# A last batch whose verdict is formed by a minimum, whose statistics and bias additions are placed between other work, and whose last block of rows is stored first

## The chip, the core and the metric

The kernel runs on one core of one Trainium2 chip. The core has five engines that run at the same time and wait for each other through semaphores: TensorE (PE, matrix products), VectorE (DVE), ScalarE (ACT), GpSimd (POOL) and SyncE (SP, which issues the DMAs of this kernel). The metric is the device time of one execution in microseconds (us), lower is better. Several executions are timed, and the median is given. One further execution is recorded by the profiler. Its span runs from the first to the last instruction, and all positions below are microseconds from the start of that span.

## The reference

The input `x` holds 32 batches of 512 rows with 512 columns in float32, `adj` is a 512x512 matrix of zeros and ones. Two layers follow each other, each a graph operation whose result is added to its input and normalised row by row.

```python
# layer 0: attention with 8 heads of 64, masked by adj
q, k, v = x @ Wq + bq, x @ Wk + bk, x @ Wv + bv
scores = einsum('bihd,bjhd->bhij', q, k) / sqrt(64)
scores += where(adj == 0, -1e9, 0)
x = layernorm(x + einsum('bhij,bjhd->bihd', softmax(scores), v))
# layer 1: neighbours summed by adj, one product with a weight, a bias
y = einsum('nm,bmd->bnd', adj, x)
x = layernorm(x + einsum('bnd,do->bno', y, weight) + bias)
# layernorm(x) = (x - mean) / sqrt(var + 1e-5) over the 512 columns
```

## The kernel before

A batch stays in SBUF as one tile of 128 partitions with four row blocks of 128 rows, called `xs` in the profile, or `xT` for the last batch. In the code it is `X[b]`, and block `c` is `X[b][:, c, :]`. Products of 512x512 matrices (the projections, and `convolve`, which multiplies the aggregated rows `YT[b]`, tile `yT`, by the weight of layer 1) are made by a scheme with seven products of quarter matrices instead of eight. `FACTORS` lists, for each of the seven, which quarter or sum of quarters stands on the left and on the right. `ORDER` and `convolution` name the order in which they are issued, for layer 1 it is 1, 2, 5, 6, 7, 3, 4. Each product is eight matmuls at line 353. The quarters A11 and A12 of the left factor are copied from PSUM, S1 is added by DVE, and S2, S3 and S4 are three POOL additions (`combine_rows`, line 318).

The order of work is written out by hand: each engine works through its instructions in program order, and the semaphores are put in from the tiles (and the parts of tiles) that an instruction reads and writes. The main loop interleaves batches. The projections of a batch run beside the attention of the one before, and layer 1 runs one batch behind again.

After the loop (line 816 on) only the end of two batches is left. With `t` = 31, the last batch, these are the steps that the change touches, in their order before:

- `rest` is layer 1 of batch 30, seven `convolve` units. A unit makes eight matmuls, after which DVE adds the PSUM bank to quarters of `X[30]` (line 534) or to a mixed sum `MIX` (line 530), and for products 6, 7 and 4 POOL adds `MIX` to a quarter (line 532, for product 4 line 537). Product 7 writes the same `MIX` tile that POOL reads for product 6.
- `ahead` is the first normalisation of batch 31. For each row block `c`, ACT normalises the block (line 430), ACT rounds it to a high part (line 491), and DVE subtracts to get the low part (line 492). Then comes the next unit of `rest`. High and low parts are the weights of `aggregate_rows`, the product with `adj`.
- `older` is the second statistics of batch 29, four pairs of `bn_stats` and `bn_aggr` on DVE (lines 415 and 416).
- `add_bias` adds the bias row of layer 1 to one block of batch 31 on POOL (line 495). It overwrites the block that the high and low parts are made from, and layer 1's products are added to it later.
- `judge` condenses three checks on sums that were gathered during the run to one number per partition: three reductions (lines 662 to 664), two comparisons (666, 667) and two multiplications (668, 669) on DVE. A small matmul at line 873 and a comparison at line 874 make of it the verdict, which decides at the end of the program whether a slower general kernel is run afterwards.
- `aggregate_rows` makes 32 matmuls (line 504) into four banks, row block by row block, and copies them to `yT`. ACT copies banks 0 and 2 (line 511), DVE copies banks 1 and 3 (line 509), and DVE adds for S1 (line 513).
- `last` is layer 1 of batch 31, its seven products interleaved with the second normalisation of batches 29 (`old`) and 30 (`seen`, `next_`) and with their stores. The end normalises and stores batch 31 block by block: blocks 0 and 1, then block 2 by ACT (line 430) and block 3 by DVE (line 887), each stored by a DMA of 256 KB on SP's queue (line 454).

Of the kernel before, what the change touches and what calls it, by code (L numbers as in the profile page):

```python
# [37 lines left out]
FP = mybir.dt.float32  # L38
# [4 lines left out]
ALU = mybir.AluOpType  # L43
AX = mybir.AxisListType
# [3 lines left out]
P = 128  # L48
# [147 lines left out]
def gnn_resnorm_kernel(tc, *args):  # L196
    nc = tc.nc
    with tc.tile_pool(name="verdict", bufs=1) as keep:
        verdict = keep.tile([1, 1], I32, name="verdict")
        fast_kernel(tc, verdict, *args)  # L200
        amiss = nc.values_load(verdict[0:1, 0:1], min_val=0, max_val=1,
                               skip_runtime_bounds_check_because="it is a comparison's result, 0 or 1")
        with tc.If(amiss > 0):
            general_kernel(tc, *args)
# [3 lines left out]
def fast_kernel(ctx: ExitStack, tc, verdict, x, adj, Wq, bq, Wk, bk, Wv, bv, W1, b1, out):  # L208
    nc = tc.nc
# [3 lines left out]
    NB = N // P  # L213
# [4 lines left out]
    consts = ctx.enter_context(tc.tile_pool(name="consts", bufs=1))  # L218
# [233 lines left out]
    def store(b, blocks=None):  # L452
        for c in blocks or ():
            nc.sync.dma_start(out[b, c * P:(c + 1) * P, :], X[b][:, c, :])
        if blocks is None:
            nc.sync.dma_start(out[b].rearrange("(c p) d -> p c d", p=P), X[b])
# [24 lines left out]
    def split_rows(b, c):  # L481

        if c > 1:
            both = work.tile([P, 2, D], FR, name="k", bufs=2)
            high, low = both[:, 0, :], both[:, 1, :]
        else:
            high = work.tile([P, D], FR, name="high")
            low = work.tile([P, D], FR, name="low")
        HIGH[b, c], LOW[b, c] = high, low
        row = X[b][:, c, :]  # L490
        nc.scalar.activation(high, row, AF.Copy)
        nc.vector.tensor_sub(low, row, high.bitcast(FP))

    def add_bias(b, c):
        nc.gpsimd.tensor_add(X[b][:, c, :], X[b][:, c, :], b1_r)
# [48 lines left out]
    def convolution(b):  # L544
        return [(convolve, b, i) for i in (1, 2, 5, 6, 7, 3, 4)] if b >= 0 else []
# [114 lines left out]
    def judge():  # L660
        seen = consts.tile([P, 3], FP, name="seen")
        nc.vector.tensor_reduce(seen[:, 0:1], sums, axis=AX.XY, op=ALU.add)
        nc.vector.tensor_reduce(seen[:, 1:2], inverses, axis=AX.XY, op=ALU.add)
        nc.vector.tensor_reduce(seen[:, 2:3], inexact, axis=AX.X, op=ALU.add)
        well = consts.tile([P, 3], FP, name="well")
        nc.vector.tensor_scalar(well[:, 0:2], seen[:, 0:2], BOUND, None, op0=ALU.is_le)
        nc.vector.tensor_scalar(well[:, 2:3], seen[:, 2:3], 0.0, None, op0=ALU.is_equal)
        nc.vector.tensor_mul(well[:, 0:1], well[:, 0:1], well[:, 1:2])
        nc.vector.tensor_mul(well[:, 0:1], well[:, 0:1], well[:, 2:3])
        return well[:, 0:1]  # L670


    def run(units):
        for unit in units:
            unit[0](*unit[1:])
# [46 lines left out]
    def norm(t, which):  # L722

        if t - which < 0:
            return []
        lo, hi = which * NB, (which + 1) * NB
        return [(square_root, t, slice(lo, hi)), (invert_root, t, slice(lo, hi))] + [
            (normalise, t, slot) for slot in range(lo, hi)]
# [4 lines left out]
    def survey(b):  # L733

        return [(statistics, b, 1, c) for c in range(NB)] if b >= 0 else []
# [81 lines left out]
    t = B - 1  # L817
    rest, last = convolution(t - 1), convolution(t)
# [5 lines left out]
        statistics(t, 0, c)  # L824
    ahead = norm(t, 0)
    run(ahead[:1] + rest[1:2] + ahead[1:2])
    for c in range(NB):
        run(ahead[2 + c:3 + c])
        split_rows(t, c)
        run(rest[2 + c:3 + c])  # L830
    run(rest[2 + NB:])
    older, seen = survey(t - 2), survey(t - 1)
    run(older)
    for c in range(NB):
        add_bias(t, c)
    well = judge()
    aggregate_rows(t)
    old = norm(t - 1, 1)
# [40 lines left out]
    for c in (2, 3):  # L879
# [6 lines left out]
    row = X[t][:, 3, :]  # L886
    nc.vector.tensor_scalar(row, row, STAT[t + 1][:, NB + 3, 0:1], RSTD[t + 1][:, NB + 3:NB + 4],
                            op0=ALU.subtract, op1=ALU.mult)
    store(t, [2, 3])


# [22 lines left out]
```

## Time and profile before

| what | value |
|---|---|
| median of 3 executions | 2749.52 us (2749.11 to 2749.98) |
| the profiled execution | 2749.17 us |
| its span | 2747.3 us |
| PE busy | 2729.7 us, 99% |
| DVE, POOL, ACT busy | 2064.8, 1903.0, 1411.4 us |
| mean granted clock of PE | 0.998 |
| start of `rest` and `ahead` in the span | about 2699 us |

The time outside the span (2749.17 less 2747.3, so 1.87 us) lies before the first and after the last instruction. A row of the timeline gives start, duration, engine, line, operation, output and input with their shapes, and in brackets how long the engine stood idle before it and what ended that. On DVE a row's duration overlaps the next one's by some 0.08 us, so that the distance from start to start is the cost of one more instruction.

### The profile page before, as it was taken

Reading aid. Unit: us, or ns where it says so; the run is one execution under the profiler, and the core shown is the slowest. Engines: PE = TensorE matmul, PEld = TensorE weight load, DVE = VectorE, ACT = ScalarE, POOL = GpSimd, SP = SyncE. Lnnn points to the kernel's source line nnn. Section 1 sums busy time; section 2 is a strip of 40 time slices with the busy share of each in tenths; the row PEclk is TensorE's granted clock in tenths of the full one; section 3 lists DMA queues with packets and bytes.
Section 4 is the critical chain, followed back from the end, with each engine's and each line's share of the span. In section 5 each row is a group of like instructions: output and inputs, shape, how many; then the busy total and the mean of one; then the engine's idle time right before and its main releaser. Section 6 shows DMA issues by size and latency. Waiting matters only on the chain.

```text
span 2747.3 us, 39383 instructions
## 1 busy us (share of the span) xinstructions
PE 2729.7 (99%) x12856; PEld 1911.3 (70%) x12856; DVE 2064.8 (75%) x3348; ACT 1411.4 (51%) x2459; POOL 1903.0 (69%) x1224
## 2 busy tenths in 40 slices
PE   9999999999999999999999999999999999999997
PEld 6676676766767767667676676676766767767666
DVE  6777777777777787777877777777777777777777
ACT  3455464554544655446555455454554644555454
POOL 4776677666867667777677676777666867667775
PEclk9999999999999999999999999999999999999999
DMA  5212211222212222122221222211222212222121
GB/s 149 32 28 62 56 29 45 57 62 57 44 30 56 61 59 54 19 57 60 60 57 23 51 59 61 56 27 47 58 62 57 43 30 56 62 58 49 25 59 50
DMA packets 592915, 142.20 MB, mean 52 GB/s; under 512 B 554560, under 2 KB 558656, under 8 KB 592704
## 3 DMA queue, kind: packets, MB, share of 16 engines
q1 hardware_dynamic: 592704, 139.63, 23.0%
q8 instruction: 103, 1.69, 0.3%
q14 instruction: 108, 0.88, 0.1%
HBM read 72.88 MB, written 33.55 MB: 39 GB/s over the span
## 4 chain that ended last, share of the span: by engine, by line
PE 98%; DVE 1%; DMA 0%; ACT 0%; issue 0%; SPq 0%; POOL 0%; DVEq 0%; ACTq 0%
PE bank L353 56%; PE bank L561 17%; PE bank L585 16%; PE bank L472 8%; PE bank L628 0%; DMA wq<-in_L_gnn_Wq_dram 0%; DVE bnst L415 0%; DVE xs L534 0%; DVE part L847 0%; PE bank L287 0%; POOL xs L532 0%; SPq L239 0%; ACT xT L430 0%; DVE stat L416 0%; DVE xT L534 0%
## 5 line engine op out<-in xcount | busy, mean ns | idle before, releaser
L565 ACT ACTIVATE e<-e 128x1024 f32<-128x1024 f32 x512 | 524.9, 1053 | 572.8 <-DVE e L563 537.5
L563 DVE SCALAR_TENSOR_TENSOR e<-gap,bank 128x512 f32<-128x512 uint8 x1024 | 617.7, 679 | 20.2 <-PE bank L561 20.2
L576 POOL TENSOR_TENSOR es<-es,e 128x1024 f32<-128x1024 f32 x256 | 618.3, 2415 | 20.1
L576 POOL TENSOR_TENSOR es<-e 128x1024 f32<-128x1024 f32 x128 | 316.2, 2470 | 328.2 <-ACT e L565 328.2
L561 PE MATMUL bank<-q,k 64*128 64x512 f32 x2048 | 463.0, 598 | 0.0
L585 PE MATMUL bank<-e,v 128*64 128x512 f32 x2048 | 453.6, 595 | 0.0
L353 PE MATMUL bank<-wv,xT 128*128 128x256 f32 x1792 | 405.4, 381 | 0.0
L353 PE MATMUL bank<-xT,wk 128*128 128x256 f32 x1792 | 402.9, 379 | 0.0
L353 PE MATMUL bank<-xT,wq 128*128 128x256 f32 x1792 | 400.8, 381 | 1.9 <-DMA wq<-in_L_gnn_Wq_dram 1.7
L353 PE MATMUL bank<-w,yT 128*128 128x256 f32 x1792 | 394.3, 380 | 3.5 <-DVE yT L509 3.5
L561 PEld LDWEIGHTS bank<-q,k 64*128 64x128 f32 x2048 | 203.4, 186 | 258.0 <-issue 152.2
L353 PEld LDWEIGHTS bank<-w,yT 128*128 128x128 f32 x1792 | 341.2, 191 | 52.0 <-DVE yT L509 3.9
L353 PEld LDWEIGHTS bank<-xT,wk 128*128 128x128 f32 x1792 | 340.2, 190 | 46.1
L353 PEld LDWEIGHTS bank<-xT,wq 128*128 128x128 f32 x1792 | 337.8, 190 | 48.9 <-issue 1.9
L353 PEld LDWEIGHTS bank<-wv,xT 128*128 128x128 f32 x1792 | 337.6, 190 | 47.6 <-DVE e L563 0.8
L644 ACT ACTIVATE rows<-rows,zero,inverse 128x64 f32<-128x64 f32 x1008 | 343.4, 427 | 4.6 <-DMA rows<-attT 4.6
L585 PEld LDWEIGHTS bank<-e,v 128*64 128x64 f32 x2048 | 141.4, 137 | 277.1 <-issue 275.7
L648 POOL TENSOR_TENSOR xs<-xs,rows 128x512 f32<-128x512 f32 x124 | 158.0, 1285 | 164.3 <-DMA xs<-in_x_dram 164.3
L565 ACT ACT_TABLE_LOAD x30 | 38.5, 1283 | 416.6 <-DVE e L563 416.6
L445 DVE TENSOR_TENSOR low<-xs,high 128x512 fp32r<-128x512 f32 x122 | 141.8, 1162 | 106.1 <-ACT high L441 106.1
L534 DVE TENSOR_TENSOR xs<-bank,xs 128x512 f32<-128x512 f32 x186 | 124.3, 682 | 96.8 <-PE bank L353 46.2
L430 ACT ACTIVATE xs<-xs,shift,rstd 128x512 f32<-128x512 f32 x248 | 181.9, 803 | 27.2 <-DVE shift L425 27.2
(128 smaller groups left out, 2963.3 us busy)
## 6 DMA issues: line engine op xcount, KB each, us to landing
rows<-attT SPq DMA_DIRECT2D x2016, 16.0 KB, 1.8
xin<-in_x_dram SPq DMA_DIRECT2D x496, 64.0 KB, 2.4
xs<-in_x_dram SPq DMA_DIRECT2D x31, 1024.0 KB, 5.1
out_dram<-xs SPq DMA_DIRECT2D x31, 1024.0 KB, 4.4
xin<-in_x_dram SPq DMA_DIRECT2D x4, 256.0 KB, 3.3
wq<-in_L_gnn_Wq_dram SPq DMA_DIRECT2D x2, 512.0 KB, 6.7
wk<-in_L_gnn_Wk_dram SPq DMA_DIRECT2D x2, 512.0 KB, 5.7
yT<-in_adj_dram SPq DMA_DIRECT2D x1, 1024.0 KB, 7.2
```

Source lines behind the costliest of these rows:

```text
L353: nc.tensor.matmul(pm[:, r, :], left[:, d, r * P:(r + 1) * P], right[:, d, :], start=(d == 0), stop=(d == 1))
L430: nc.scalar.activation(row, row, AF.Identity, bias=SHIFT[t][:, slot:slot + 1], scale=RSTD[t][:, slot:slot + 1])
L445: nc.vector.tensor_sub(LOW[b, d], cols, HIGH[b, d].bitcast(FP))
L472: nc.tensor.matmul(pm.rearrange("p a n -> p (a n)"), part, adjT[:, n % NB, :], start=(n == 0), stop=(n == 2 * NB - 1))
L534: nc.vector.tensor_add(block, pm, block)
L561: nc.tensor.matmul(ps[s], keys[:, j * P:(j + 1) * P], queries, start=True, stop=True)
L563: nc.vector.scalar_tensor_tensor(e[:, s, :], gap[:, j, :], NEG * root, ps[s], op0=ALU.mult, op1=ALU.add)
L565: nc.scalar.activation(e, e, AF.Exp, scale=1.0 / root)
L576: nc.gpsimd.tensor_add(ES[b, hp], ES[b, hp] if j > 1 else E[b, hp, 0], E[b, hp, j])
L585: nc.tensor.matmul(po[s * HD:(s + 1) * HD, :], values, e[:, s, :], start=(j == 0), stop=(j == NB - 1))
L644: nc.scalar.activation(part, part, AF.Identity, bias=zero, scale=inverse[:, c, s:s + 1])
L648: nc.gpsimd.tensor_add(cols, cols, ROWS.pop((b, hp)))
```

## The change

- `judge` makes one reduction with a minimum over its three columns in place of the two multiplications, into a fourth column of the tile `well`.
- The additions of bias to the four blocks of batch 31 are issued within the loop over `c`: for block 0 right after the low part, for blocks 1 to 3 after the unit of `rest` that follows the low part.
- Two of the four statistics of batch 29 are issued in the loop at `c` = 2, after the low part and ahead of product 7. The other two stay after the last unit of `rest`.
- The last two stores are issued in the order block 3, block 2.

```diff
-        well = consts.tile([P, 3], FP, name="well")
+        well = consts.tile([P, 4], FP, name="well")
         nc.vector.tensor_scalar(well[:, 0:2], seen[:, 0:2], BOUND, None, op0=ALU.is_le)
         nc.vector.tensor_scalar(well[:, 2:3], seen[:, 2:3], 0.0, None, op0=ALU.is_equal)
-        nc.vector.tensor_mul(well[:, 0:1], well[:, 0:1], well[:, 1:2])
-        nc.vector.tensor_mul(well[:, 0:1], well[:, 0:1], well[:, 2:3])
-        return well[:, 0:1]
+        nc.vector.tensor_reduce(well[:, 3:4], well[:, 0:3], axis=AX.X, op=ALU.min)
+        return well[:, 3:4]
...
     run(ahead[:1] + rest[1:2] + ahead[1:2])
+    older, seen = survey(t - 2), survey(t - 1)
+
     for c in range(NB):
         run(ahead[2 + c:3 + c])
         split_rows(t, c)
+        if c == 0:
+            add_bias(t, c)
+        if c == 2:
+            run(older[:2])
         run(rest[2 + c:3 + c])
-    run(rest[2 + NB:])
-    older, seen = survey(t - 2), survey(t - 1)
-    run(older)
-    for c in range(NB):
-        add_bias(t, c)
+        if c > 0:
+            add_bias(t, c)
+    run(rest[2 + NB:] + older[2:])
     well = judge()
     aggregate_rows(t)
...
-    store(t, [2, 3])
+    store(t, [3, 2])
```

## The prediction

> **What bounds the kernel now.** The page came first: PE is busy 99% of 2747.3 us at a mean clock of 0.998, so only places where PE stands still or runs slowly can give anything before PE's end, and after it the chain of the last batch. The waits of PE over the whole run name one such place at the end:
>
> ```profile
> PE bank L353 <- DVE yT L509: 3.5, 1, 3.5
> ```
>
> The columns are total, count and longest. It is one wait. The chain of work that ended last (start, duration, what) shows what PE waits for, namely `judge`, of which two multiplications of one column take 2.4 us:
>
> ```profile
> 2719.50 0.48 DVE well L666
> 2719.98 0.06 DVE well L667
> 2720.04 1.16 DVE well L668
> 2721.20 0.02 issue
> 2721.22 1.18 DVE well L669
> 2722.41 0.61 DVE yT L509
> 2723.02 0.04 issue
> 2723.07 10.16 PE bank L353 x38
> ```
>
> The timeline of DVE and POOL tells why such small instructions are slow, and gives the prices used below:
>
> ```profile
> 2711.91 1.68 POOL L532 TENSOR_TENSOR xs<-xs,mix 128x512 f32<-128x512 f32 x1 [8.48 <-DVE mix L530]
> ...
> 2713.62 0.69 DVE L530 TENSOR_TENSOR mix<-bank,mix 128x512 f32<-128x512 f32 x1 [1.19 <-POOL xs L532]
> ...
> 2717.44 4.96 POOL L495 TENSOR_TENSOR xT<-xT,b_r 128x512 f32<-128x512 f32 x4
> ...
> 2719.28 0.16 DVE L663 TENSOR_REDUCE seen<-inverses 128x1 f32<-128x16 f32 x1
> ...
> 2719.90 0.14 DVE L667 TENSOR_SCALAR well<-seen 128x1 f32<-128x1 f32 x1
> ...
> 2722.33 0.68 DVE L509 COPY yT<-bank 128x512 f32<-128x512 f32 x1
> ```
>
> The four bias additions run back to back from 2717.44, 1.24 us apart, so they end near 2718.7, 2719.9, 2721.2 and 2722.4. Lines 666, 668 and 669 end at 2719.98, 2721.20 and 2722.40: each waited for the POOL addition in flight. The reductions and line 667 did not. DVE also stood idle 1.19 us before line 530 (product 7 behind POOL's line 532).
>
> Last, the granted clock of PE, by stage (length, busy of the engines, then PEclk, DMA share, GB/s):
>
> ```profile
> 2719.00:2721.00 2.00, 0.58 (x3) 0.17 (x1) 1.97 (x8) 0.32 (x1) 2.00 (x2) 1.00 0.00 0
> ...
> 2723.00:2724.00 1.00, 0.93 (x4) 0.86 (x5) 1.00 (x4) 0.00 (x0) 0.00 (x0) 1.00 0.00 0
> 2724.00:2725.00 1.00, 1.00 (x5) 0.77 (x4) 0.27 (x1) 0.18 (x1) 0.59 (x1) 0.67 0.00 0
> 2725.00:2726.00 1.00, 1.00 (x4) 0.82 (x3) 0.48 (x1) 0.60 (x2) 1.00 (x2) 0.50 0.00 0
> 2726.00:2727.00 1.00, 1.00 (x4) 0.82 (x3) 0.97 (x4) 0.04 (x1) 1.00 (x2) 0.50 0.00 0
> 2727.00:2728.00 1.00, 1.00 (x4) 0.79 (x4) 0.96 (x3) 1.00 (x2) 1.00 (x1) 0.62 0.00 0
> ```
>
> After the gap the clock falls to a half for some 3 us, which costs 0.33 + 0.50 + 0.50 + 0.38 = 1.7 us of PE's work.
>
> **What the Trainium skill says.** "SBUF — State Buffer", Who interferes with whom: DVE and GpSimd share a pair of ports as an exclusive lock; a DVE instruction with two SBUF inputs, or a one-input one in a two-port mode, waits for a running GpSimd instruction that reads SBUF, while `tensor_reduce` never does. The trace agrees: the multiplications waited 1.1 us each, the reductions took 0.14 to 0.16 us under a busy POOL. "VectorE: DVE Perf Modes", Mode 2×_2P: the two-port mode wants an even outermost dimension (or an odd one equal on both sides). Line 666 (two columns) waited; line 667 (one column) did not, so here the measurement decides. "TensorE: Matmul & The Clock Gate", What's actually happening: after an idle window of about 3.4 us the clock is halved. The 3.5 us gap and the 0.50 after it fit.
>
> **The change, part by part.** Durations are start to start: 0.60 us for a DVE operation on 512 columns, 0.80 for a statistics pair (2716.02 to 2716.84), 1.24 for POOL. One that finds the pair taken starts when it is released.
>
> *Bias of block 0.* It can start at 2709.51, after the low part ends at 2709.43, and ends at 2710.78. The low part of block 1, due at 2710.55, waits for it and ends at 2711.33 instead of 2711.23: 0.10 us later, and so is line 530 of product 6 (ends 2711.93). POOL's line 532 waits for DVE's low part of block 2, as before (the 1.68 above), and ends at 2713.69; bias 1 behind it ends at 2714.93.
>
> *Two statistics ahead of product 7.* They fill 2712.45 to 2714.05. Line 530 needed POOL's 2713.69, so 1.60 us of work replaces a wait that was 1.19: it then runs to 2714.73. If that cover were gone they would simply cost their 1.60 here and save 1.60 later.
>
> *Low part of block 3.* It is ready at 2714.65 but bias 1 holds the pair to 2714.93: it ends at 2715.50 against 2714.91. PE reaches block 3's matmuls after 24 of 32, 2711.31 + 24 x 0.233 = 2716.9, so 1.4 us of cover remain.
>
> *POOL afterwards.* The addition of product 7 starts when the low part lets go (2715.41) and ends at 2716.65, bias 2 at 2717.89, bias 3 at 2719.13, line 537 of product 4 at 2720.37. Line 537 comes later than before (2717.48); its reader is the statistics of batch 30, more than 5 us further on.
>
> *DVE afterwards.* Products 3 and 4 take 2715.42 to 2716.62, the other two statistics end at 2718.22, three reductions and an issue bring line 666 to 2718.47. There it meets bias 3 and waits until 2719.13, 0.66 us. Its price is thus 0 to 1.24 us by where it falls in a POOL addition; my sum gives 0.66. Line 667 and the minimum follow at 0.12 each (667 to 668 was 0.12), so the copy of line 509 starts near 2719.35 instead of 2722.33. The minimum is a form not seen before; the reductions of line 664 (0.07 to 0.12 start to start) and the page's word that it never waits bound it at 0.07 and, if it did wait, 1.24.
>
> *PE.* The matmul after the copy starts 0.74 us behind it (2722.33 to 2723.07), so at 2720.09. The gap shrinks from 3.50 to 0.5 us, too short for the clock to fall.
>
> *What is late next.* From the copy on DVE sets the pace, not PE: it is busy almost without a break from 2725.5 to 2735, its line 530 for product 6 starts at 2733.24 long after product 6 was made, and product 3's addition at 2735.37 waited 0.60 for the POOL addition behind that. PE's own product 3 ended at 2735.28, so both arrived together. Ahead of that DVE is tied to POOL's S2 to S4 additions: line 425 waited for the second of them to end, and these follow DVE's copies by a fixed distance (POOL is free from 2720.37, they are due at 2721.4). So everything behind the copy moves by 2722.33 - 2719.35 = 2.98 us, stores of batches 29 and 30 on SP's queue included, and the 1.7 us of clock become slack of PE.
>
> *Stores.* Block 3 is ready at 2741.08 (DVE, line 887), block 2 at 2741.53 (ACT). Before, SP issued at 2741.55 and 2741.98. Now it issues block 3 at about 2741.1 and block 2 at 2741.55, 0.43 us earlier for the last. But instruction fetches (the rows q8 and q14 of the DMA part of the page) run on some of the same DMA engines at that moment[...]. Between 0 and 0.43, I take 0.2.
>
> *Sum:* 2.98 + 0.2 = 3.2 us. The profiled execution took 2749.17 (span 2747.3 and 1.87 around it), so 2746.0 for it; the median shown is 0.35 above it, so 2746.3.
>
> **Rivals.** A change of 0.2% is 5.5 us (about what a measurement of this kernel can tell from no change): a faster time outside it would be below 2744.0.
>
> 1. *One POOL addition more.* Line 666 or the minimum misses bias 3 and waits for line 537, to 2720.37. For it: DVE has only 0.66 us in hand, and line 667 may take the pair too. Against: it did not before. Gain 3.2 - 1.24 = 2.0, so 2747.5.
> 2. *PE is the bound to the end.* Then the clock counts: 3.0 + 1.7 + 0.2 = 4.9, so 2744.6. For it: PE and POOL arrived within 0.1 us at product 3. Against: DVE's unbroken chain.
> 3. *Starvation.* POOL keeps the pair while it has work, and the low part of block 3 waits for two additions more, to 2718.0. Then the copy comes near 2721.3, gain 1.2, 2748.3. Against: lines 666 and 668 got in at the next boundary with POOL's queue full.
> 4. *Slower.* `well` grows by 4 bytes per partition, which can move the tiles laid out after it. If operands at other addresses made each of PE's 12,856 matmuls 3.2 us / 12,856 = 0.25 ns longer, the gain would be gone; 0.5 ns gives 2752.7. Nothing in the profile shows a cost by address.
> 5. *Nothing.* The copy is held by something not seen, 2749.5. Against: its bank is complete near 2718.3, between ACT's copies at 2717.84 and 2718.72.
>
> **How the numbers follow.** My forecast (2745.3 to 2747.0) 0.66; rival 1 0.13; rival 2 0.10; rival 3 0.05; rival 4 0.03; rival 5 0.03. The range 2744.8 to 2748.2 takes in the forecast, rival 1, part of 2 and part of 3. Faster by over 0.2% is the lower edge of rival 2, 0.04; slower by over 0.2% the upper edge of rival 4, 0.01; the rest, 0.95, lies within.
>
> **What would show it.** PE's wait for line 509 at 0.3 to 0.8 us, a granted clock of 1.00 in the twelve us after it, no row of `well` but line 666 above 0.2 us, no idle time of DVE before product 7's line 530, the copy near 2719.35, the last DMA issue near 2738.6. A PE wait of 1.5 us or more speaks for rivals 1 or 3; a tail from the copy to the last DVE instruction shorter than before (18.75 us, 2722.33 to 2741.08) for rival 2; PE's matmuls in the main loop longer than before for rival 4. Wrong would be a copy that starts earlier while the end does not.

## The result and the profile after

The changed kernel takes 2745.82 us (median of 22 executions, 2744.52 to 2747.74) against 2750.36 us for the kernel before (22 executions, 2748.33 to 2753.43). The ratio is 0.9983, with a 95% interval from 0.9978 to 0.9989, so 4.5 us less, with 3.0 to 6.1 us inside the interval. The forecast was 2746.3 us and 3.2 us less. The profiled execution took 2744.69 us, its span 2742.9 us.

The waits of PE over the whole run, of the changed kernel (total, count, longest):

```profile
PE bank L353 <- DVE yT L509: 0.5, 1, 0.5
```

Before, this wait was 3.5 us. The chain of work that ended last, of the changed kernel (start, duration, what), shows the judgement without its long rows. Line 668 is now the minimum. Behind the copy the chain leaves PE after the six matmuls that complete product 1, passes ACT's copy of it (line 524) and is mostly DVE's from there on, where it had stayed with PE for 10 us:

```profile
2717.43 0.69 DVE well L666
2718.12 0.07 DVE well L667
2718.19 0.02 issue
2718.21 0.16 DVE well L668
2718.37 0.61 DVE yT L509
2718.98 0.04 issue
2719.02 1.58 PE bank L353 x6
2720.60 0.02 issue
2720.62 0.61 ACT mix L524
```

The timeline of POOL and DVE of the changed kernel, the rows that answer to those shown of before:

```profile
2710.95 1.67 POOL L532 TENSOR_TENSOR xs<-xs,mix 128x512 f32<-128x512 f32 x1 [1.23 <-DVE mix L530]
...
2713.01 0.67 DVE L530 TENSOR_TENSOR mix<-bank,mix 128x512 f32<-128x512 f32 x1
...
2713.83 1.76 POOL L532 TENSOR_TENSOR xs<-xs,mix 128x512 f32<-128x512 f32 x1
...
2717.40 0.72 DVE L666 TENSOR_SCALAR well<-seen 128x2 f32<-128x2 f32 x1
2718.03 0.14 DVE L667 TENSOR_SCALAR well<-seen 128x1 f32<-128x1 f32 x1
2718.21 0.16 DVE L668 TENSOR_REDUCE well<-well 128x1 f32<-128x3 f32 x1
2718.28 0.68 DVE L509 COPY yT<-bank 128x512 f32<-128x512 f32 x1
```

DVE no longer stands idle before line 530 of product 7, the minimum takes 0.16 us while POOL works, and of the judgement only line 666 waits for POOL, once. The granted clock by stage (length, busy of the engines, PEclk, DMA share, GB/s) stays at full speed behind the short gap:

```profile
2718.00:2719.00 1.00, 0.51 (x3) 0.11 (x1) 0.97 (x5) 0.25 (x1) 1.00 (x2) 1.00 0.00 0
2719.00:2720.00 1.00, 0.98 (x5) 0.88 (x6) 1.00 (x3) 0.00 (x0) 0.32 (x1) 1.00 0.00 0
2720.00:2721.00 1.00, 1.00 (x6) 0.90 (x5) 0.22 (x1) 0.38 (x1) 0.63 (x1) 1.00 0.00 0
2721.00:2722.00 1.00, 1.00 (x7) 0.87 (x6) 0.68 (x2) 0.40 (x2) 1.00 (x2) 1.00 0.00 0
2722.00:2723.00 1.00, 1.00 (x6) 0.88 (x5) 0.97 (x4) 0.08 (x1) 1.00 (x2) 1.00 0.00 0
```

Positions in two profiles can't be compared from the start of the span, because the work ahead of the change differs from execution to execution by about as much as the change is worth. T0, the start of the first low part of batch 31 (line 492), lies at 2708.74 us in the first profile of before, at 2707.68 us in that of the changed kernel, and between 2707.68 and 2711.75 us over all profiles of this study. A part of this spread is the clock at the start of the run: in the four profiles with T0 beyond 2710 us (e1, e4, e6 and the second one of the changed kernel) the granted clock falls to a half between 8 and 16 us, in the other ten it does not. From T0 the two stand like this (the length of a span is read to 0.1 us, so its end is good to 0.05 us):

| from T0, us | before | changed | difference |
|---|---|---|---|
| copy of line 509 starts | 13.59 | 10.60 | 2.99 |
| from there to the end of DVE's last instruction | 18.75 | 18.68 | 0.07 |
| from there to the end of the span | 6.22 | 5.94 | 0.28 |
| end of the span | 38.56 | 35.22 | 3.34 |

The spans of these two profiles differ by 4.4 us; 1.06 us of that is the difference in T0, ahead of anything the change touches.

### The profile page after: what moved, and what is told of

Read it like the earlier page. It is cut to its first block, busy times and chain, and to the rows that moved or that the text cites. A ratio compares the mean times of both kernels' runs of the same rounds, so it can differ in the third digit from the quotient of the medians.

```text
span 2742.9 us, 39381 instructions
## 1 busy us (share of the span) xinstructions
PE 2728.6 (99%) x12856; PEld 1911.0 (70%) x12856; DVE 2063.2 (75%) x3347; ACT 1411.1 (51%) x2459; POOL 1903.8 (69%) x1224
## 3 DMA queue, kind: packets, MB, share of 16 engines
q8 instruction: 103, 1.69, 0.3%
## 4 chain that ended last, share of the span: by engine, by line
PE 98%; DVE 1%; DMA 0%; ACT 0%; issue 0%; SPq 0%; POOL 0%; DVEq 0%; ACTq 0%
PE bank L353 56%; PE bank L561 17%; PE bank L585 16%; PE bank L472 8%; PE bank L628 0%; DVE bnst L415 0%; DMA wq<-in_L_gnn_Wq_dram 0%; DVE xT L534 0%; DVE xs L534 0%; DVE part L850 0%; DVE stat L416 0%; DVE mix L530 0%; PE bank L287 0%; SPq L239 0%; ACT xT L430 0%
```

## The experiments

Each was profiled once, and all but the last also timed against the kernel before. The table gives what the profile of each shows. "Tail" is from the start of the copy to the end of DVE's last instruction, "end" is the end of the span from T0, and the last column is the median less that of the kernel before in the same comparison. The intervals of these differences reach some 2 us to each side, so the verdicts on single parts rest on the positions.

| kernel | copy | PE's wait | tail | last DVE to end | end | median difference |
|---|---|---|---|---|---|---|
| before | 13.59 | 3.5 | 18.75 | 6.22 | 38.56 | |
| changed | 10.60 | 0.5 | 18.68 | 5.94 | 35.22 | -4.5 |
| e1, minimum only | 11.40 | 1.3 | 18.83 | 6.26 | 36.49 | -2.7 |
| e2, moves only | 11.76 | 1.7 | 18.69 | 6.42 | 36.87 | -2.7 |
| e3, stores only | 13.59 | 3.5 | 20.03 | 5.79 | 39.41 | +0.2 |
| e4, changed, old stores | 10.61 | 0.5 | 18.68 | 6.28 | 35.57 | -4.4 |
| e5, biases only | 11.97 | 1.9 | 18.70 | 6.46 | 37.13 | -2.3 |
| e6, statistics only | 12.69 | 2.6 | 19.89 | 6.37 | 38.95 | -1.2 |
| e7, before, judgement early | 10.49 | 0.4 | 18.51 | 6.41 | 35.41 | -4.1 |
| e8, changed, judgement early | 9.52 | none | 19.19 | 6.02 | 34.73 | -5.0 |
| e9, e8 and one pair moved | 9.52 | none | 18.40 | 6.43 | 34.35 | -5.6 |
| e10, before, PE kept busy | 13.60 | none | 19.94 | 6.39 | 39.93 | +0.2 |
| changed again | 10.60 | 0.5 | 18.69 | 6.17 | 35.46 | -4.2 |
| before again | 13.59 | 3.5 | 19.91 | 6.48 | 39.98 | |

**e1, the minimum alone.**

```diff
-        well = consts.tile([P, 3], FP, name="well")
+        well = consts.tile([P, 4], FP, name="well")
...
-        nc.vector.tensor_mul(well[:, 0:1], well[:, 0:1], well[:, 1:2])
-        nc.vector.tensor_mul(well[:, 0:1], well[:, 0:1], well[:, 2:3])
+        nc.vector.tensor_reduce(well[:, 3:4], well[:, 0:3], axis=AX.X, op=ALU.min)
...
```

> Positions are counted from T0, the start of the first low part of batch 31 (line 492): in the kernel before the copy of line 509 starts at T0 + 13.59 us and the span ends at T0 + 38.56, in the changed kernel at + 10.60 and + 35.22. Here only the minimum takes the place of the two multiplications; biases, statistics and stores stay. Theory (each multiplication waited for one POOL addition, the minimum waits for none): line 666 still waits and ends at T0 + 11.24, the copy starts at + 11.4, PE waits 1.3 us, its clock stays at 1.00, the span ends at + 36.4, 2.2 us less than before. Rival (the minimum waits for POOL too): copy at + 12.5, 1.1 us less.

The copy started at 11.40 and PE waited 1.3 us, and the clock stayed at 1.00, all as the theory had it. The minimum took 0.16 us under a busy POOL. The rival (the minimum waits too) falls.

**e2, the moves alone,** with both multiplications kept and the old order of stores:

```diff
+    older, seen = survey(t - 2), survey(t - 1)
...
+        if c == 0:
+            add_bias(t, c)
+        if c == 2:
+            run(older[:2])
         run(rest[2 + c:3 + c])
+        if c > 0:
+            add_bias(t, c)
-    run(rest[2 + NB:])
+    run(rest[2 + NB:] + older[2:])
```

> The biases and the two statistics are moved, the two multiplications and the old order of stores stay. Theory (the multiplications cost what POOL makes them wait): line 668 waits for POOL's last addition (line 537, ends at T0 + 11.64), line 669 finds POOL idle and takes 0.1 us, so the copy starts at T0 + 11.75 and the span ends at + 36.7, 1.8 us less than before. Rival (a multiplication of one column costs 1.16 us by itself): copy at + 12.9, 0.7 us less.

The timeline of POOL and DVE of e2:

```profile
2719.10 1.26 POOL L537 TENSOR_TENSOR xs<-xs,mix 128x512 f32<-128x512 f32 x1
...
2719.20 1.18 DVE L668 TENSOR_TENSOR well<-well 128x1 f32<-128x1 f32 x1
2720.41 0.16 DVE L669 TENSOR_TENSOR well<-well 128x1 f32<-128x1 f32 x1
```

Two multiplications of the same size, one after the other: the first takes 1.18 us and ends within 0.02 us of POOL's last addition (2720.36), the second takes 0.16 us because POOL is idle. The price belongs to POOL's work and not to the instruction. The copy at 11.76 is the forecast 11.75.

**e3 and e4, the order of the stores,** alone and taken out of the changed kernel:

```diff
-    store(t, [2, 3])
+    store(t, [3, 2])
```

> Only block 3 is stored ahead of block 2. The copy stays at T0 + 13.59. Theory: the last DMA is issued 0.43 us earlier against the end of DVE's last instruction, and of that 0.2 to 0.35 us reach the end of the span: it ends at T0 + 38.25. Rival (fetches of instructions on the same DMA engines set the end): 38.56, no gain.

> The changed kernel with the old order of the last two stores. Theory: copy at T0 + 10.60 as in the changed kernel, PE waits 0.5 us, the span ends at T0 + 35.5, 0.3 us later than the changed kernel. Rival (the order of stores gives nothing): 35.2.

Behind DVE's last instruction the nine profiles with the old order need 6.22 to 6.48 us, 6.37 in the mean. The five with the new order need 5.94, 5.79, 6.02, 6.43 and 6.17, 6.07 in the mean. The means differ by 0.3 us, but single profiles overlap, so a gain from the order is likely and not shown. The times don't resolve it: e3's ratio is 1.0 with an interval of 0.9991 to 1.0009, some 2.5 us to both sides. The end of e3's span missed both expectations for another reason, its tail of 20.03 us, which is taken up below.

**e5, the biases alone,** and **e6, the statistics alone,** each with the multiplications and stores of before. e5 has the two `add_bias` places of e2's diff without `older[:2]`, e6 has `older[:2]` at `c` = 2 and the biases behind the statistics as before.

> Only the biases are moved into the loop; statistics, multiplications and stores stay as before. Theory: the low part of block 3 waits for bias 1 and ends 0.55 us later than before, line 666 comes at T0 + 11.3 and waits for POOL's last addition to + 11.65, then POOL is idle and the multiplications take 0.1 us each: copy at T0 + 11.95, 1.6 us less than before at the end. Rival (the biases delay the low parts and PE): copy after T0 + 13.6 or a PE wait at line 504.

> Only the two statistics are moved ahead of product 7; biases, multiplications and stores stay as before. Theory: the statistics fill the wait of 1.19 us before line 530, line 666 comes at T0 + 9.5, waits for one bias, and each multiplication waits for one more: copy at T0 + 12.7, 0.9 us less than before at the end. Rival (the statistics only change places): copy at + 13.6, nothing gained.

Both copies came where they were expected (11.97 for 11.95, 12.69 for 12.7). In e5 both multiplications found POOL idle (0.16 us each). In e6 all three waited, and still the copy was 0.9 us early because the wait of 1.19 us before line 530 was filled. e6's end was expected at 37.7 and came at 38.95, again with a long tail. The gains of the parts don't add: e1's 2.19 and e2's 1.83 us of the copy make 4.0, while both together give 2.99, because e2 already lets the second multiplication find POOL idle.

**e7, the judgement early.** The kernel before with one line moved, multiplications included:

```diff
     run(ahead[:1] + rest[1:2] + ahead[1:2])
+    well = judge()
     for c in range(NB):
...
-    well = judge()
     aggregate_rows(t)
```

> The kernel before with one change: the whole judgement, multiplications included, is issued ahead of the loop, where DVE waits 1.6 us for ACT's first high part and POOL is idle. Theory: no row of it takes over 0.2 us, T0 does not move, and the copy starts when the four statistics end, at T0 + 10.5; the span ends 3.1 us earlier than before, as with nearly the whole change. Rival (the instructions are slow by themselves): lines 668 and 669 take 1.16 us each and T0 comes some 1.2 us later against the shift of line 425.

The timeline of DVE of e7:

```profile
2707.78 0.17 DVE L666 TENSOR_SCALAR well<-seen 128x2 f32<-128x2 f32 x1
2707.85 0.15 DVE L667 TENSOR_SCALAR well<-seen 128x1 f32<-128x1 f32 x1
2707.98 0.16 DVE L668 TENSOR_TENSOR well<-well 128x1 f32<-128x1 f32 x1
2708.18 0.16 DVE L669 TENSOR_TENSOR well<-well 128x1 f32<-128x1 f32 x1
2709.19 0.69 DVE L492 TENSOR_TENSOR low<-xT,high 128x512 fp32r<-128x512 f32 x1 [0.85 <-ACT high L491]
```

No row of the judgement is longer than 0.17 us, and DVE still waits 0.85 us for ACT behind it, so it costs nothing there: T0 lies 1.77 us behind the start of line 425 (2707.42), as in the kernel before (2706.97 to 2708.74). Moving this one call gives the copy at 10.49, as much as the whole change with its four edits, and the same median (2745.89 us).

**e8, the changed kernel with the judgement early,** the same move on top of the change.

> The changed kernel with the judgement ahead of the loop. Theory: DVE is free for the copy at T0 + 9.5 and the bank is complete at about + 9.6, so the copy starts at + 9.6, PE has no wait, and the span ends 0.9 to 1.0 us earlier than in the changed kernel, at T0 + 34.3, since DVE sets the pace behind the copy. Rival (PE sets the end): the end moves by 0.5 us at most, the wait that PE has left in the changed kernel.

The copy came at 9.52 and PE had no wait, but the end came 0.5 us earlier than in the changed kernel, not 0.9 to 1.0. The timeline of DVE shows why:

```profile
2718.79 0.69 DVE L509 COPY yT<-bank 128x512 f32<-128x512 f32 x1
2719.89 0.42 DVE L513 TENSOR_TENSOR yT<-bank,yT 128x256 f32<-128x256 f32 x1 [0.40 <-ACT yT L511]
2720.23 0.68 DVE L509 COPY yT<-bank 128x512 f32<-128x512 f32 x1
```

DVE is now ahead of ACT's copy of bank 2, which follows PE's last matmuls with `adj`. The number was the rival's, its cause, the wait that PE had left, was not. POOL's additions, which line 425 waits for, follow DVE's copies, and these now follow PE's product with `adj` and ACT: the additions start at 12.11 us from T0, for 12.69 in the changed kernel.

**e9, one statistics pair of batch 30 moved into DVE's idle time,** on top of e8.

```diff
     aggregate_rows(t)
+    run(seen[:1])
...
-    beside = {1: old + seen[:2], 2: seen[2:] + next_[:2], 5: next_[2:4], 6: next_[4:]}
+    beside = {1: old + seen[1:2], 2: seen[2:] + next_[:2], 5: next_[2:4], 6: next_[4:]}
```

> The changed kernel with the judgement ahead of the loop, and one statistics pair of batch 30 issued right behind DVE's copies, where DVE stood idle 0.91 us for ACT's copy of product 1. Theory (DVE sets the pace behind the copies): the pair fits into the idle time, line 425 still waits for POOL's second addition, and the end comes 0.8 us earlier than without it, at T0 + 33.9, so 1.3 us ahead of the changed kernel. Rival (PE or POOL sets the end): T0 + 34.7, no gain from it.

The timeline of DVE of e9:

```profile
2720.13 0.68 DVE L415 BATCH_NORM_STATS2 bnst<-xs 128x6 f32<-128x512 f32 x1
2720.85 0.18 DVE L416 BATCH_NORM_AGGREGATE stat<-bnst 128x2 f32<-128x6 f32 x1
2721.13 0.69 DVE L534 TENSOR_TENSOR xT<-bank,xT 128x512 f32<-128x512 f32 x1
2721.74 0.17 DVE L424 RECIPROCAL rstd<-rstd 128x4 f32<-128x4 f32 x1
2721.94 0.94 DVE L425 SCALAR_TENSOR_TENSOR shift<-stat,rstd 128x4 f32<-128x4 f32 x1
```

The pair fits ahead of line 534 without an idle stretch, and DVE's last instruction ends 0.79 us earlier than in e8 (tail 18.40 for 19.19). So with PE at full clock the way from the copies to DVE's last instruction leads over DVE and the POOL additions that line 425 waits for, and PE does not bound the kernel to the end, as rival 2 of the prediction had it. But PE is not far from that way: ahead of line 534 DVE waits for ACT's copy of product 1 and so for PE (0.91 us in e8, 1.09 in the changed kernel, 1.25 before), and the pair filled just this wait. The end missed its expectation, 34.35 for 33.9: of the 0.79 us only 0.38 reached the end of the span, since the stretch behind DVE's last instruction took 6.43 us in this profile and 6.02 in e8's. Its median, 2744.34 us, lies 5.6 us below that of before (ratio 0.998, 0.9972 to 0.9988) and 1.45 us below the changed kernel in the same comparison. It is the fastest kernel of the study.

**The long tails: before once more, and PE kept busy.** The first three profiles with a long wait of PE differ in their tails: before 18.75, e3 20.03, e6 19.89. One more profile of the unchanged kernel before:

> The kernel before once more, for the moment at which its clock falls. Theory: PE waits 3.5 us and the copy starts at T0 + 13.59 as in each profile of it; the half clock begins at another distance from the wait than 5 us, between 3 and 6.5 us behind the wait's start, and the stretch from the copy to DVE's last instruction is 18.7 us when it begins late and up to 20.0 when it begins at once. Rival (a fixed distance): again 4.8 us behind the wait's start and 18.7 us.

Its granted clock by stage:

```profile
2722.00:2723.00 1.00, 0.06 (x1) 0.06 (x1) 1.00 (x3) 0.00 (x0) 0.27 (x1) 0.96 0.00 0
2723.00:2724.00 1.00, 1.00 (x3) 0.82 (x4) 1.00 (x3) 0.00 (x0) 0.00 (x0) 0.50 0.00 0
2724.00:2725.00 1.00, 1.00 (x4) 0.82 (x3) 0.15 (x1) 0.00 (x0) 0.71 (x1) 0.50 0.00 0
2725.00:2726.00 1.00, 1.00 (x4) 0.82 (x3) 0.00 (x0) 0.09 (x1) 1.00 (x2) 0.50 0.00 0
2726.00:2727.00 1.00, 1.00 (x5) 0.83 (x5) 0.40 (x1) 0.69 (x2) 1.00 (x2) 0.83 0.00 0
```

and its timeline of DVE:

```profile
2726.60 0.69 DVE L534 TENSOR_TENSOR xT<-bank,xT 128x512 f32<-128x512 f32 x1 [2.46 <-ACT mix L524]
2727.21 0.17 DVE L424 RECIPROCAL rstd<-rstd 128x4 f32<-128x4 f32 x1
2727.41 0.62 DVE L425 SCALAR_TENSOR_TENSOR shift<-stat,rstd 128x4 f32<-128x4 f32 x1
```

The first profile of before has these rows in the same place:

```profile
2724.41 3.72 POOL L318 TENSOR_TENSOR yT<-yT 128x512 f32<-128x512 f32 x3 [2.02 <-DVE yT L513]
...
2725.52 0.69 DVE L534 TENSOR_TENSOR xT<-bank,xT 128x512 f32<-128x512 f32 x1 [1.25 <-ACT mix L524]
2726.12 0.17 DVE L424 RECIPROCAL rstd<-rstd 128x4 f32<-128x4 f32 x1
2726.33 0.60 DVE L425 SCALAR_TENSOR_TENSOR shift<-stat,rstd 128x4 f32<-128x4 f32 x1
```

In the new profile the clock is at a half from the first matmul behind the wait (2722.94), in the first one it fell some 1.3 us after it. The six matmuls that complete product 1 then take longer, ACT's copy (line 524) starts 3.70 us behind the copy of line 509 in place of 2.49, and DVE waits 2.46 us instead of 1.25. Line 425 therefore misses the end of POOL's second addition and waits for the third. In the first profile it started 0.56 us ahead of that end (2726.33, and the second of the three additions ends near 2726.89). So in these profiles the price of a later product 1 is a step, nothing or about one POOL addition. The tail is 19.91 us, 1.16 longer. The same unchanged code thus ends at 38.56 or at 39.98 from T0. The theory holds, and a fixed distance is refuted: the half clock began 4.8 us behind the start of PE's wait in the first profile and some 3.5 us behind it here.

The other test was to take the wait away from PE alone:

```diff
     aggregate_rows(t)
+    idle = bank(2, half)
+    for _ in range(13):
+        nc.tensor.matmul(idle[:, 0, :], ident, w1[:, 0, 0, :], start=True, stop=True)
```

> The kernel before with 13 matmuls more, whose result nothing reads, between the 32 of line 504 and product 1: PE then waits about 0.8 us in place of 3.5, while DVE's copy stays at T0 + 13.59. Theory (after the long wait the clock falls at a moment that differs from execution to execution; where it falls at once it costs about 1.3 us at the end, where it falls later nothing): the clock stays at 1.00, the span ends at T0 + 38.4 to 38.6, and the median of the times is 0.4 to 1.0 us below that of the kernel before. Rival (the clock never reaches the end): the same median as before, within 0.3 us.

It did not test what it was meant to. Each of the 13 calls makes two matmuls at 0.216 us, so the filling took 5.6 us instead of the 2.8 that I had reckoned, and held up product 1 itself. ACT's copy came 4.18 us behind the copy, the tail was 19.94 at a clock of 1.00, and the median was the same as before. That is the rival's number, but with product 1 held up it doesn't speak for the rival. On the share of slow clocks in the times of before it says nothing directly. It does show that a late product 1 costs 1.2 us in the tail by itself, whatever makes it late.

**The changed kernel again,** beside e9 and e10:

> The changed kernel once more, beside the others. Theory: copy at T0 + 10.60, end at T0 + 35.2, clock 1.00; 3.3 us ahead of the kernel before where its clock cost nothing, 4.6 where it fell at once, so 3.6 to 4.3 in the median. Rival (the gain is the 3.2 us of the sum alone): 3.2 us.

The copy came at 10.60, the tail was 18.69, the clock did not fall before PE's end, and the end was at 35.46. The median was 4.2 us below before.

## Why the prediction was right, and where a term was missing

- *Biases and the low parts.* Right: the low part of block 1 ended 0.10 us later from T0 (2.59 for 2.49), bias 1 ended at 6.19 as reckoned, the low part of block 3 at 6.74 (6.76 reckoned), and PE had no wait at line 504.
- *Statistics ahead of product 7.* Right: line 530 started at 5.33 (5.31) without idle time. Alone they gave 0.9 us (e6).
- *Line 666 and the minimum.* Right: line 666 came at 9.72 (9.73), waited for bias 3 to 10.44 (10.39), and the minimum cost 0.07 us. The copy started at 10.60, for 10.61 reckoned. Rivals 1, 3 and 5 did not come true: line 666 did not wait for line 537, POOL alternated with DVE at each end of an addition (the 1.76 us of POOL's line 532 above is such a turn), and nothing unseen held the copy. Of rival 4 nothing was seen: the matmuls of line 353 for the projections last 379 to 381 ns in both profiles, and e7, with `well` as before, gains as much as the change. On line 667 the prediction put the condition too widely: the Trainium skill, "VectorE: DVE Perf Modes", Mode 2×_2P, speaks of the outermost dimension that is not of size one, and a single column has none. So the 0.14 us of line 667 beside a busy POOL does not contradict that section.
- *What is late next.* The tail kept its length (18.68 for 18.75), so DVE's chain and its tie to POOL's additions are right, and e9 shows it by a gain of 0.79 us for 0.80 us of DVE work moved. What the prediction left out is how near PE's product 1 is to this chain (next point).
- *Stores.* 0.2 us of a possible 0.43 was taken, and 0.3 us is the difference of the means over the profiles, which overlap.
- *The clock.* This is the step that was incomplete. It put the 1.7 us of slow clock down as slack of PE, from one profile in which the clock fell after product 1 was nearly made. But line 534 and with it line 425 wait for product 1, and line 425 had only 0.56 us in hand before it would miss POOL's second addition. In two of three profiles with PE's wait of 3.5 us (e3, which has before's code up to the stores, and before again) the clock fell by the time PE went on, and then 1.2 to 1.3 us are added to the tail. The change takes this away as well, since its wait of 0.5 us let the clock fall in none of its profiles. So from T0 the gain is 3.3 us against an execution of before with a late fall and about 4.6 against one with an early fall.
- *How often it falls early* was not counted. The medians speak for an early fall as the more frequent case. For each kernel whose profile shows no fall before PE's end, the end from T0 can be set against the 38.56 of before's first profile, and the median against that of before: e1 2.07 and 2.7, e2 1.69 and 2.7, e4 2.99 and 4.4, e5 1.43 and 2.3, e7 3.15 and 4.1, e8 3.83 and 5.0, e9 4.21 and 5.6, the changed kernel 3.34 and 4.5, again 3.10 and 4.2. The median differs by more each time, by 1.1 us in the mean of the nine; and e10, whose end is 1.37 us later than that of before's first profile, has before's median. The nine share four medians of before, and each single interval is wide (that of the change, 3.0 to 6.1 us, holds the 3.2 of the forecast). The pattern of the clock in the last section allows an estimate of its own: if the grid found there lies anywhere with equal chance, if a fall needs 1.7 to 2.1 us idle in one interval, and with the 0.56 us in hand, a wait of 3.49 us makes line 425 miss POOL's second addition in six to seven executions of ten. At 1.2 us each that is 0.7 to 0.9 us on average. So the missing term is an expected loss of some 0.7 to 1.1 us in the kernel before that its one profile did not contain. Its mechanism is what the profiles show, its size is an estimate.
- *Rival 2 and luck.* The gain of 4.5 us lies nearer to rival 2's 4.9 than to the forecast's 3.2. Its path, PE as the bound to the end, did not hold, but its clock did count, through product 1. That the forecast time of 2746.3 us came within 0.5 us of 2745.82 was luck in part: the gain was 1.3 us larger than forecast, while the kernel before, 2749.52 us in the three executions that the forecast started from, has a median of 2750.36 over 22.

## What to carry to other kernels

An instruction of one column can cost nearly as much as a GpSimd addition of 512 columns beside it: the multiplications of two SBUF operands took 1.16 to 1.18 us there and 0.16 us with GpSimd idle, while the reductions took 0.14 to 0.16 us in either place. Look for where such an instruction stands and in which form, and move it to a place where GpSimd is idle and its own engine waits anyway (e7 reached with one moved line what the change reached with four edits). A wait of TensorE can cost more than its length if it slows the clock, and one profile doesn't show how much, because the moment of the fall changes from execution to execution. Compare profiles from a common event just ahead of the change: here the start of the same work varied by 4 us, about as much as the effect.

## What was not expected of the hardware

- The prediction reckoned with an idle window of about 3.4 us, but less is enough. After a wait of PE of 2.6 us (e6) the clock was at a half soon after the first matmul behind it; after waits of 1.3, 1.7 and 1.9 us (e1, e2, e5) it stayed at full speed. With the same wait of 3.5 us the half clock began 2.7 (e3), 3.5 (before again) and 4.8 us (before) behind the wait's start.
- The moments are less arbitrary than they look. In the clock records of all fourteen traces, every stretch at full or half clock between the first and the last change is a whole multiple of 3.413 us long: 1 or 2 of them at half clock, 1, 2, 4 or 794 to 802 at full clock. So the clock changes on a grid, and where the grid lies against T0 differs from execution to execution. The table has, for the stretch around PE's wait, the grid interval in which PE stood idle longest:

| profile | interval, us from the start of the span | PE idle in it, us | clock behind it |
|---|---|---|---|
| before again | 2719.51 to 2722.92 | 3.41 | half |
| e3 | 2718.02 to 2721.43 | 2.70 | half |
| e6 | 2722.02 to 2725.44 | 2.58 | half |
| before | 2720.94 to 2724.35 | 2.13 | half |
| e2 | 2718.23 to 2721.65 | 1.66 | full |
| e5 | 2717.91 to 2721.33 | 1.41 | full |
| e1 | 2720.93 to 2724.34 | 1.29 | full |

The idle time within an interval, and not the length of the wait, goes with the fall. It is not one sharp bound: near the start of the run the clock also fell behind intervals with 1.81 to 2.14 us idle (1.81 in e4), and behind PE's end in the changed kernel it did not with 1.99.

- The half clock lasted one interval (3.41 us) in both profiles of before, in which PE was busy all the while (idle for 0.02 us at most), but two (6.83 us) in e3, where 0.78 us of PE's wait fell into the first.
- DVE and POOL took turns where one waited for the other: no row read here waited for more than one instruction of the other engine, even with POOL's additions queued back to back.
